# Perceiver layers: how the softmax sums of the last two head groups are joined in the two context attentions

## The chip, the cores and the metric

The kernel runs on one core of one Trainium2 chip. The time is that of the device, in microseconds (us), for one execution; where several executions were timed, the median is given. The profile comes from one more execution, which the hardware profiler recorded.

## What is computed

Two perceiver layers work on 512 tokens of width 512 and on a context of 8192 rows of width 512, of which a key mask leaves a part. Each layer adds to x a cross attention from the tokens to the context (16 heads of width 32), a self attention, and a mixture of eight experts with two chosen. The change is in the cross attention alone, here called the context attention:

```python
x = x + _L0_xattn_ref(_layernorm(x, axis=-1), ctx_1024, mask_BxS2_bk0, ...)
x = x + _L0_attn_ref(_layernorm(x, axis=-1), ...)
x = x + _L0_ffn_ref(_layernorm(x, axis=-1), ...)
x = x + _L1_xattn_ref(_layernorm(x, axis=-1), ctx_1024, ctx_1024, mask_Bx1xSxS2_ik1, ...)
...
attn = jnp.einsum('bhid,bjhd->bhij', q, k)
attn = jnp.where(padding_mask[:, None, None, :], attn, -jnp.inf)
p = jax.nn.softmax(attn, axis=-1)
ctx = jnp.einsum('bhij,bjhd->bihd', p, v).reshape(b, s1, c)
out = ctx @ Wo.T + bo
```

## The kernel before

`attend_slots` does the context attention of one layer; it is built twice, once for each layer. The 16 heads make four groups of four heads (g = 0 to 3), and the keys that the mask leaves are gathered into n = 15 slots of 128 keys. The main part is a loop over 60 rounds, `at = 15 * g + i`, one for each group and slot. In this document a round is called by `at`: round 44 is the last slot of the third group (g = 2), rounds 45 to 59 are the last group (g = 3).

A round makes four score tiles, one for each head (`score`, TensorE, then `subtract`, which adds the negated row maxima, also on TensorE), and their exponentials (`exp`, ScalarE), which go into one tile `pT` of 128 keys by 4 heads by 512 queries. `accumulate` then multiplies the `pT` of an earlier round with the values (`acc`, TensorE). In the rounds before 41 the score maxima of the next group are worked out as well (`compare`, `take`); from round 41 on there are none, and `accumulate(2)` serves the round before the last one. For the first three groups each `acc` is a PSUM tile of its own, and VectorE adds it into `o` in SBUF (line 1052). For the last group all 15 slots sum up in one PSUM tile.

The softmax also needs the sum of `pT` over all keys. `add_up` adds the `pT` of up to four rounds into a tile `four`: on GpSimd (POOL) for the first three groups, on VectorE (DVE) for the last. What is left are the parts of a group: five for each of the first three groups (`four` of rounds 0-3, 4-7, 8-11, 12-13, and the `pT` of round 14), six for the last (three `four` and three `pT`). `denominators` multiplies each part with ones on TensorE, four matrix products for the four heads (line 1072), and they add up in the PSUM tile `den`. ScalarE turns `den` into its inverse as exp(-ln(den)) (lines 1078 and 1083; 202 and 203 in the last group).

`fillers` is a list of steps with the round from which they are due; one is taken at the end of each round. For the first three groups it holds `denominators` three rounds after the group's end, `divide` one later (GpSimd multiplies `o` with the inverse and adds the value bias, lines 1084 and 1086), and `outputs`, which multiplies `o` with the output weights (line 889) and has VectorE add the result to x (line 895). For the third group the outputs come in rounds 57 and 58.

The PSUM tiles of scores, `acc`, `den` and `ops` take their buffers in turn from seven (four tagged s, three tagged m), and before the last group from an eighth (tagged a, where the last group's `acc` then stays):

```python
k.tags = cycle("smsmsmsa")
...
                k.tags = cycle("smsmsms")
                acc = k.sums[g] = pacc.tile([P, S], F32, name="acc", tag="acc")
```

A tile can be written only when the last reader of the tile that held its buffer before is done. Each engine takes its instructions in the order in which the program was laid out. `pT` has five buffers, `four` five, `o` two.

Of the kernel before, what the change touches and what calls it, by code (L numbers as in the profile page):

```python
# [11 lines left out]
F32 = mybir.dt.float32  # L12
# [4 lines left out]
AF = mybir.ActivationFunctionType  # L17
ALU = mybir.AluOpType
# [3 lines left out]
P = 128  # L22
S = 512
# [6 lines left out]
NG = 4  # L30
# [35 lines left out]
def tile_perceiver(  # L66
# [5 lines left out]
    nc = tc.nc  # L72
# [127 lines left out]
    def inverse(to, src):  # L200

        nc.scalar.activation(to, src, AF.Ln)
        nc.scalar.activation(to, to, AF.Exp, scale=-1.0)
# [581 lines left out]
    def in_quads(pool, psum, pacc, qT, wo, bv, late, splits=None):  # L785
# [4 lines left out]
        k = SimpleNamespace(tags=cycle("ms"), ones32=ones[:, 0:HD], most={}, shifts={}, sums={}, o={}, d={}, bufs={"s": 3, "m": 3}, rowwise=False, negs={}, direct=(0,), later=(), last=NT - 1, lag=False, between=None)  # L790
# [54 lines left out]
        def begin(g):  # L845
            k.sums[g] = [pacc.tile([P, S], F32, name=name, tag=name) for name in ("acc", "den")]

        def divided(g, r, d, acc, den):
            inverse(d[:, r], den)
            nc.vector.tensor_tensor(k.o[g][:, r], acc, d[:, r], ALU.mult)  # L850
            if bv is not None:

                nc.scalar.activation(k.o[g][:, r], k.o[g][:, r], AF.Identity, bias=bv[:, g : g + 1])

        def finish_part(g, r, acc, den):

            if g not in k.o:
                k.o[g] = late().tile([P, S], F32, name="o", tag="o", bufs=2)
            divided(g, r, late().tile([P, S], F32, name="d", tag="d", bufs=1), acc, den)

        def finish(g, pieces=1):

# [31 lines left out]
                else:  # L894
                    nc.vector.tensor_tensor(x[:, t, :], x[:, t, :], ps, ALU.add)

        k.tile_s, k.subtract, k.shift_of = tile_s, subtract, shift_of
        k.begin, k.finish, k.finish_part, k.outputs, k.quotient = begin, finish, finish_part, outputs, quotient
        return k

# [18 lines left out]
    def attend_slots(pool, psum, pacc, kT, vN, qT, kbias, krow, wo, bv, late, keys, settle, values, unit, more, early, aside, beside, extra, plan, tail, phase=None):  # L919
# [6 lines left out]


        k = in_quads(pool, psum, pacc, qT, wo, bv, late, nc.gpsimd)
        k.bufs["s"] = 4
        k.rowwise = True  # L930
# [4 lines left out]
        tile_s, subtract, shift_of = k.tile_s, k.subtract, k.shift_of  # L935
        n = SLOTS

        def score(g, i, h, ps, stop):
            nc.tensor.matmul(  # L939
                ps, lhsT=kT[HD * h : HD * (h + 1), g, i * P : (i + 1) * P], rhs=qT[HD * h : HD * (h + 1), g, :],  # L940
                start=True, stop=stop,
            )

        whole = n * P // S
        rest = n * P - whole * S
# [80 lines left out]
        parts, dens = {g: [] for g in range(NG)}, {}  # L1026
# [3 lines left out]
        def accumulate(lag):  # L1030

            if len(behind) < lag:
                return
            g, i, pT = behind.pop(0)
            alone = g < NG - 1
            if alone:
                acc = tile_s(name="acc")
            elif i == 0:
                k.tags = cycle("smsmsms")
                acc = k.sums[g] = pacc.tile([P, S], F32, name="acc", tag="acc")  # L1040
            else:
                acc = k.sums[g]
            for h in range(GH):
                nc.tensor.matmul(  # L1044
                    acc[HD * h : HD * (h + 1), :], lhsT=vN[:, i, g * P + HD * h : g * P + HD * (h + 1)],
                    rhs=pT[:, h, :], start=alone or i == 0, stop=alone or i == n - 1,
                )
            if alone and i == 0:
                k.o[g] = late().tile([P, S], F32, name="o", tag="o", bufs=2)
                nc.scalar.copy(k.o[g], acc)  # L1050
            elif alone:
                nc.vector.tensor_tensor(k.o[g], k.o[g], acc, ALU.add)  # L1052

        def add_up(g, i, pT):

            engine = nc.gpsimd if g < NG - 1 else nc.vector
            if i % 4 == 0 or i >= (n - 1 if g < NG - 1 else (n - 1) // 4 * 4):
                parts[g].append(pT)
                return
            to = parts[g][-1]  # L1060
            if i % 4 == 1:
                to = late().tile([P, GH, S], F32, name="four", tag="four", bufs=5)
            engine.tensor_tensor(to, parts[g][-1], pT, ALU.add)  # L1063
            parts[g][-1] = to

        def denominators(g, which, end):

            for j in which:
                if j == 0:
                    dens[g] = tile_s(name="den")  # L1070
                for h in range(GH):
                    nc.tensor.matmul(
                        dens[g][HD * h : HD * (h + 1), :], lhsT=k.ones32, rhs=parts[g][j][:, h, :],
                        start=(j == 0), stop=(j == end - 1),
                    )
            if g < NG - 1:
                d = late().tile([P, S], F32, name="d", tag="d", bufs=1)
                nc.scalar.activation(d, dens[g], AF.Ln)
                dens[g] = d

        def divide(g):

            nc.scalar.activation(dens[g], dens[g], AF.Exp, scale=-1.0)
            nc.gpsimd.tensor_tensor(k.o[g], k.o[g], dens[g], ALU.mult)

            nc.gpsimd.tensor_scalar(k.o[g], k.o[g], bv[:, g : g + 1], None, ALU.add)

        def exp(pT, h, i, ps):
            nc.scalar.activation(pT[:, h, :], ps, AF.Exp, bias=kbias[:, i : i + 1])  # L1089

        for at in range(NG * n):
            g, i = divmod(at, n)
            mg, mi = divmod(at + n + lead, n)
            pT = late().tile([P, GH, S], F32, name="pT", tag="pT", bufs=5)
            if mg < NG:

                w, m = {}, {}
                for now, then in (((0, 1), (2, 3)), ((2, 3), (0, 1))):
                    for h in now:
                        w[h] = tile_s()  # L1100
                        score(g, i, h, w[h], False)
                    for h in then:
                        m[h] = tile_s(name="scm")
                        compare(mg, mi, h, m[h])
                    for h in now:
                        subtract(g, h, w[h])
                    for h in now:
                        exp(pT, h, i, w[h])
                    for h in then:
                        take(mg, mi, h, m[h])  # L1110
                accumulate(1)
                if mi == n - 1:
                    for j, f in zip((1, 3), shift_of(mg)):
                        fillers.append((at + j, f))
            else:
                tiles = [tile_s() for _ in range(GH)]
                for h in range(GH):
                    score(g, i, h, tiles[h], False)
                for h in range(GH):
                    subtract(g, h, tiles[h])  # L1120
                for h in range(GH):
                    exp(pT, h, i, tiles[h])
                accumulate(2)
            add_up(g, i, pT)
            if i == n - 1 and g < NG - 1:
                fillers.extend((
                    (at + 3, lambda g=g: denominators(g, range(len(parts[g])), len(parts[g]))),
                    (at + 4, lambda g=g: divide(g)),
                    (at + (13 if g == NG - 2 else 10), lambda g=g: k.outputs(g, (0, 1))),
                    (at + (14 if g == NG - 2 else 11), lambda g=g: k.outputs(g, (2, 3))),  # L1130
                ))
            behind.append((g, i, pT))
            fillers.sort(key=lambda f: f[0])
            if fillers and fillers[0][0] <= at:
                fillers.pop(0)[1]()
            if g == NG - 1 and i >= n - 2:

                lone = n - (n - 1) // 4 * 4
                whole = (n - 1) // 4
                end = whole + lone  # L1140
                denominators(g, range(0, whole - 1) if i == n - 2 else range(whole - 1, end - 2), end)
        accumulate(1)
        denominators(NG - 1, range(end - 2, end), end)
        accumulate(1)
        for _, f in fillers:
            f()
        for i in range(2):
            r = slice(i * S // 2, (i + 1) * S // 2)
            k.finish_part(NG - 1, r, k.sums[NG - 1][:, r], dens[NG - 1][:, r])
        k.outputs(NG - 1, range(NT))  # L1150

    def columns(pool, vector, tag):
# [1519 lines left out]
    for i in range(2):  # L2672
        nc.vector.tensor_tensor(worst, worst, overs[:, i : i + 1], ALU.max)
    n = nc.values_load(
        worst, min_val=0, max_val=2 * NKT,
        skip_runtime_bounds_check_because="a count of at most NKT, or that and NKT",
    )
    with tc.If(n > SLOTS):

        load_x()  # L2680
        with tile_pool(name="osb", bufs=1) as op:
            for i in range(2):
                o = op.tile([P, S], F32, name=f"osb{i}", tag=f"osb{i}")
# [5 lines left out]
        with tile_pool(name="osb1", bufs=1) as op:  # L2689
            for i in range(2):  # L2690
                o = op.tile([P, S], F32, name=f"osb1{i}", tag=f"osb1{i}")
# [113 lines left out]
```

## Time and profile before

| what | value |
|---|---|
| three timed runs | 1433.89, 1439.09, 1439.64 us (median 1439.09) |
| the profiled execution | 1441.17 us, of which the profile's span is 1439.5 us |
| mean granted TensorE clock | 0.992 |
| TensorE (PE) busy | 1402.9 us, 97% of the span |
| VectorE (DVE), ScalarE (ACT), GpSimd (POOL) busy | 696.0, 582.7, 425.4 us |
| context attention of layer 0, rounds 41 to 59 | about 335 to 394 us of the span |
| the same rounds in layer 1 | about 1095.6 to 1154.7 us |

Times in the views of the profile are microseconds from the span's start. A timeline row gives start, duration, engine, line, operation, tiles (output <- inputs), shape and count; in brackets stands how long the engine was idle before it and what ended that. A row of several instructions gives the time from the first's start to the last's end. A fp32 matrix product shows as two records, so the four products of one part are "x8". PE is the matrix products, PEld the weight loads beside them. PEclk is the clock that TensorE was granted, as a share of full speed.

### The profile page before, as it was taken

To read this page: it belongs to the slowest core of one execution; us is meant where nothing else is said; L and a number is where in the kernel's file an instruction comes from. 1 tells how busy PE (TensorE), PEld (TensorE's weight loads), DVE (VectorE), ACT (ScalarE), POOL (GpSimd) and SP (SyncE) were. 2 spreads that over 40 slices of the span, in tenths; PEclk is the share of its full clock that TensorE was granted. 3 is DMA by queue.
4 is the path that set the end of the run, shared out by engine and by line. 5 is a ranking of instruction groups with operands and counts; after the bars stand their busy time and mean duration, and the time that the engine had idled before them with its cause. 6 is when DMAs were issued, how large, how long until landed. Compare 5 with 4: busy or idle time off the path is not lost. (4 is left out here: it accounts for less than half of the span.)

```text
span 1439.5 us, 24959 instructions
## 1 busy us (share of the span) xinstructions
PE 1402.9 (97%) x9797; PEld 859.5 (60%) x9797; DVE 696.0 (48%) x1985; ACT 582.7 (40%) x1168; POOL 425.4 (30%) x359
## 2 busy tenths in 40 slices
PE   7989999999999999999999999999999999999997
PEld 3434444443244548999999766644434235499993
DVE  5558598985523524111111226768986525741112
ACT  2657476667723253111111121166667832411211
POOL 2151078987011110200001110058988010120002
PEclk9999999999999999999999999999999999999999
DMA  8554200000050005987888450000000050077574
GB/s 248 150 194 147 74 31 1 2 1 1 5 209 1 16 16 188 390 303 261 276 280 297 154 181 23 30 1 2 1 1 2 1 190 1 10 271 288 203 263 156
DMA packets 94267, 175.15 MB, mean 122 GB/s; under 512 B 5496, under 2 KB 32182, under 8 KB 92348
## 3 DMA queue, kind: packets, MB, share of 16 engines
q1 hardware_dynamic: 87004, 151.43, 31.4%
q0 software_dynamic: 6416, 19.94, 3.9%
q10 hardware_dynamic: 720, 2.10, 0.4%
q8 instruction: 79, 1.29, 0.4%
q14 instruction: 48, 0.39, 0.1%
HBM read 162.72 MB, written 9.68 MB: 120 GB/s over the span
## 5 line engine op out<-in xcount | busy, mean ns | idle before, releaser
L1089 ACT ACTIVATE pT<-sc,kbias 128x512 f32<-128x512 f32 x480 | 288.3, 707 | 95.9 <-PE sc L800 86.5
L968 DVE CUSTOM_DVE_ANT_0 masked<-scm,krowb 128x512 f32<-128x512 f32 (+2 forms) x400 | 213.8, 591 | 39.8 <-PE scm L957 38.2
L939 PE MATMUL sc<-qTf,kTf 32*128 32x512 f32 x960 | 216.6, 621 | 1.5 <-DVE tops L968 1.5
L2363 PE MATMUL hps<-tokens,w 128*128 128x160 f32 (+11 forms) x1408 | 193.3, 293 | 0.0
L957 PE MATMUL scm<-kTf,qTf 32*128 32x512 f32 (+2 forms) x800 | 188.9, 539 | 0.0
L2363 PEld LDWEIGHTS hps<-tokens,w 128*128 128x128 f32 x1408 | 184.1, 191 | 2.7 <-issue 1.0
L2384 PE MATMUL y<-hT,w 128*128 128x160 f32 (+11 forms) x1280 | 174.6, 295 | 0.0
L2384 PEld LDWEIGHTS y<-hT,w 128*128 128x128 f32 x1280 | 168.1, 191 | 2.5 <-issue 0.8
L1063 POOL TENSOR_TENSOR four<-four,pT 128x2048 f32<-128x2048 f32 x36 | 163.9, 4553 | 1.6
L939 PEld LDWEIGHTS sc<-qTf,kTf 32*128 32x128 f32 x960 | 73.6, 183 | 95.6 <-DVE tops L968 42.5
L1044 PE MATMUL acc<-pT,vNf 128*32 128x512 f32 x960 | 127.8, 604 | 0.0
L1063 POOL TENSOR_TENSOR four<-pT 128x2048 f32<-128x2048 f32 x24 | 109.3, 4555 | 54.1 <-ACT pT L1089 54.1
L968 DVE CUSTOM_DVE_ANT_0 masked<-sc,krowb 128x512 f32<-128x512 f32 (+2 forms) x176 | 98.4, 614 | 55.4 <-PE sc L957 55.0
L2615 DVE TENSOR_TENSOR hT<-sg,hps 128x264 f32<-128x264 f32 (+7 forms) x64 | 27.9, 436 | 192.4 <-ACT sg L2614 191.0
L2614 ACT ACTIVATE sg<-hps 128x264 f32<-128x264 f32 (+7 forms) x64 | 25.3, 396 | 174.5 <-PE hps L2363 169.7
L957 PEld LDWEIGHTS scm<-kTf,qTf 32*128 32x128 f32 x800 | 86.1, 184 | 15.4 <-issue 6.2
L800 PE MATMUL sc<-shift,ones 3*128 3x512 bf16 (+3 forms) x544 | 93.3, 368 | 0.0
L2415 POOL DMA_DIRECT2D answers_d<-yb x17 | 9.6, 564 | 238.7 <-ACT yb L2402 233.0
L1052 DVE TENSOR_TENSOR o<-o,acc 128x512 f32<-128x512 f32 x84 | 57.3, 682 | 20.5 <-PE acc L1044 20.5
L1044 PEld LDWEIGHTS acc<-pT,vNf 128*32 128x32 f32 x960 | 19.3, 108 | 70.3 <-DVE tops L968 34.7
L1233 PE MATMUL pv<-wkvf,cslot 128*128 128x512 f32 x120 | 55.4, 611 | 3.1 <-DMA wq<-in_L_xattn_WqT 1.9
L1421 PE MATMUL pk<-cslot,wkf 128*128 128x256 f32 (+1 forms) x256 | 55.5, 370 | 0.0
(391 smaller groups left out, 1833.0 us busy)
## 6 DMA issues: line engine op xcount, KB each, us to landing
w<-in_L_ffn_W SPq DMA_DIRECT2D x94, 1024.0 KB, 5.3
mi<-in_mask SPq DMA_DIRECT2D x32, 512.0 KB, 4.6
cslot<-in_ctxT SPq DMA_DIRECT2D x40, 256.0 KB, 4.0
answers_d<-yb POOLq DMA_DIRECT2D x13, 256.0 KB, 4.6
answers_d<-zero POOLq DMA_DIRECT2D x9, 256.0 KB, 3.1
wkvf<-in_L_xattn_WkvT SPq DMA_DIRECT2D x8, 256.0 KB, 6.6
wof<-in_L_xattn_WoT SPq DMA_DIRECT2D x2, 1024.0 KB
wide<-in_L_attn_wk SPq DMA_DIRECT2D x4, 512.0 KB, 5.9
```

Source lines behind the costliest of these rows:

```text
L800: nc.tensor.matmul(ps, lhsT=ones16[r, :], rhs=k.shifts[g][r, 0:w], start=start, stop=stop)
L939: nc.tensor.matmul(ps, lhsT=kT[HD * h : HD * (h + 1), g, i * P : (i + 1) * P], rhs=qT[HD * h : HD * (h + 1), g, :], start=True, stop=stop,)
L957: nc.tensor.matmul(ps[:, at : at + w], lhsT=qT[HD * h : HD * (h + 1), g, t * P : (t + 1) * P], rhs=kT[HD * h : HD * (h + 1), g, lo : lo + ...
L968: nc.vector.tensor_tensor_reduce(masked[:, 0:w], ps[:, at : at + w], krow[:, lo : lo + w], 1.0, -BIG, ALU.add, ALU.max, accum_out=tops[g % ...
L1044: nc.tensor.matmul(acc[HD * h : HD * (h + 1), :], lhsT=vN[:, i, g * P + HD * h : g * P + HD * (h + 1)], rhs=pT[:, h, :], start=alone or i ...
L1052: nc.vector.tensor_tensor(k.o[g], k.o[g], acc, ALU.add)
L1063: engine.tensor_tensor(to, parts[g][-1], pT, ALU.add)
L1089: nc.scalar.activation(pT[:, h, :], ps, AF.Exp, bias=kbias[:, i : i + 1])
L1233: last = nc.tensor.matmul(ps.rearrange("p (g n) -> p g n", g=NG), lhsT=src[:, c, s % 2, :], rhs=wkv[:, :, c, i * P : (i + 1) * P], start=( ...
L1421: end = nc.tensor.matmul(ps[:, j], lhsT=wk[:, g, c], rhs=src[:, c], start=(c == 0), stop=(c == NC - 1))
L2363: end = nc.tensor.matmul(ps[:, j, 0:k], lhsT=w1[:, c, f * P : (f + 1) * P], rhs=tokens[:, c, starts[r] : starts[r] + k], start=(c == 0), s ...
L2384: nc.tensor.matmul(accs[0][:, d, 0:k], lhsT=w2[:, f, d * P : (d + 1) * P], rhs=hT[:, f, 0:k], start=(c == 0 and f == 0 and d % 2 == 0), st ...
```

## The change

For the third group (g = 2): right after its last round, VectorE adds the last `pT` into the fourth `four` and then the first `four` into the second (`join`), so that three parts are left in place of five. Its `denominators` are due four rounds after the group's end in place of three, and its `divide` five in place of four. Its quotient is multiplied on VectorE and its bias added on ScalarE, where both were GpSimd's.

For the last group: VectorE joins the first two `four` after slot 7, the sum and the third `four` after slot 11, and adds the `pT` of slot 12 as well, so that three parts are left in place of six. `denominators` no longer runs in rounds 58 and 59; all of it comes at the end, the two lone `pT` before the last `acc` and the `four` after it. The inverse is taken of both halves first, and then both are multiplied.

In the layout of the built program nothing else moves. On VectorE the two joins of the third group stand after the first of its last three additions of `acc` into `o`, and ahead of the other two.

```diff
         def add_up(g, i, pT):
-            engine = nc.gpsimd if g < NG - 1 else nc.vector
-            if i % 4 == 0 or i >= (n - 1 if g < NG - 1 else (n - 1) // 4 * 4):
+            final = g == NG - 1
+            if i % 4 == 0 and not (final and i >= n - 3) or i >= n - (2 if final else 1):
                 parts[g].append(pT)
                 return
...
-            engine.tensor_tensor(to, parts[g][-1], pT, ALU.add)
+            (nc.vector if final else nc.gpsimd).tensor_tensor(to, parts[g][-1], pT, ALU.add)
             parts[g][-1] = to
+            if final and i in (n // 2, n - 4):
+                join(g, 1, 0)
+
+        def join(g, to, of):
+            ins = nc.vector.tensor_tensor(parts[g][to], parts[g][to], parts[g][of], ALU.add)
+            parts[g].pop(of)
+            return ins
...
         def divide(g):
             nc.scalar.activation(dens[g], dens[g], AF.Exp, scale=-1.0)
+            if g == NG - 2:
+                nc.vector.tensor_tensor(k.o[g], k.o[g], dens[g], ALU.mult)
+                nc.scalar.activation(k.o[g], k.o[g], AF.Identity, bias=bv[:, g : g + 1])
+                return
             nc.gpsimd.tensor_tensor(k.o[g], k.o[g], dens[g], ALU.mult)
...
             add_up(g, i, pT)
+            if i == n - 1 and g == NG - 2:
+                joined = join(g, 3, 4)
+                with tc.issue_after(joined.ins):
+                    join(g, 1, 0)
             if i == n - 1 and g < NG - 1:
+                rest = 4 if g == NG - 2 else 3
                 fillers.extend((
-                    (at + 3, lambda g=g: denominators(g, range(len(parts[g])), len(parts[g]))),
-                    (at + 4, lambda g=g: divide(g)),
+                    (at + rest, lambda g=g: denominators(g, range(len(parts[g])))),
+                    (at + rest + 1, lambda g=g: divide(g)),
...
-            if g == NG - 1 and i >= n - 2:
-                lone = n - (n - 1) // 4 * 4
-                whole = (n - 1) // 4
-                end = whole + lone
-                denominators(g, range(0, whole - 1) if i == n - 2 else range(whole - 1, end - 2), end)
         accumulate(1)
-        denominators(NG - 1, range(end - 2, end), end)
+        denominators(NG - 1, (1, 2), True, False)
         accumulate(1)
+        denominators(NG - 1, (0,), False, True)
...
         for i in range(2):
-            r = slice(i * S // 2, (i + 1) * S // 2)
-            k.finish_part(NG - 1, r, k.sums[NG - 1][:, r], dens[NG - 1][:, r])
+            inverse(d[:, r[i]], dens[NG - 1][:, r[i]])
+        for i in range(2):
+            k.divided(NG - 1, r[i], d[:, r[i]], k.sums[NG - 1][:, r[i]])
         k.outputs(NG - 1, range(NT))
```

More of the change, by code (lines that the diff above doesn't have):

```diff
@@ L846, in begin, with divided @@
             k.sums[g] = [pacc.tile([P, S], F32, name=name, tag=name) for name in ("acc", "den")]
-        def divided(g, r, d, acc, den):
-            inverse(d[:, r], den)
-            nc.vector.tensor_tensor(k.o[g][:, r], acc, d[:, r], ALU.mult)
+        def divided(g, r, d, acc):
+            nc.vector.tensor_tensor(k.o[g][:, r], acc, d, ALU.mult)
             if bv is not None:
@@ L858, in finish_part @@
                 k.o[g] = late().tile([P, S], F32, name="o", tag="o", bufs=2)
-            divided(g, r, late().tile([P, S], F32, name="d", tag="d", bufs=1), acc, den)
+            d = late().tile([P, S], F32, name="d", tag="d", bufs=1)
+            inverse(d[:, r], den)
+            divided(g, r, d[:, r], acc)
         def finish(g, pieces=1):
@@ L895, in outputs @@
                     nc.vector.tensor_tensor(x[:, t, :], x[:, t, :], ps, ALU.add)
-        k.tile_s, k.subtract, k.shift_of = tile_s, subtract, shift_of
+        k.tile_s, k.subtract, k.shift_of, k.divided = tile_s, subtract, shift_of, divided
         k.begin, k.finish, k.finish_part, k.outputs, k.quotient = begin, finish, finish_part, outputs, quotient
@@ L1062, in add_up, with denominators @@
                 to = late().tile([P, GH, S], F32, name="four", tag="four", bufs=5)
-            engine.tensor_tensor(to, parts[g][-1], pT, ALU.add)
+            (nc.vector if final else nc.gpsimd).tensor_tensor(to, parts[g][-1], pT, ALU.add)
             parts[g][-1] = to
-        def denominators(g, which, end):
+            if final and i in (n // 2, n - 4):
[4 more added lines that the diff above has]
+            return ins
+        def denominators(g, which, first=True, last=True):
+            if first:
+                dens[g] = tile_s(name="den")
             for j in which:
-                if j == 0:
-                    dens[g] = tile_s(name="den")
                 for h in range(GH):
@@ L1073, in denominators @@
                         dens[g][HD * h : HD * (h + 1), :], lhsT=k.ones32, rhs=parts[g][j][:, h, :],
-                        start=(j == 0), stop=(j == end - 1),
+                        start=first and j == which[0], stop=last and j == which[-1],
                     )
@@ L1135, in attend_slots @@
                 fillers.pop(0)[1]()
-            if g == NG - 1 and i >= n - 2:
-                lone = n - (n - 1) // 4 * 4
-                whole = (n - 1) // 4
-                end = whole + lone
-                denominators(g, range(0, whole - 1) if i == n - 2 else range(whole - 1, end - 2), end)
         accumulate(1)
-        denominators(NG - 1, range(end - 2, end), end)
+        denominators(NG - 1, (1, 2), True, False)
         accumulate(1)
+        denominators(NG - 1, (0,), False, True)
         for _, f in fillers:
             f()
+        r = slice(0, S // 2), slice(S // 2, S)
+        d = late().tile([P, S], F32, name="d", tag="d", bufs=1)
+        k.o[NG - 1] = late().tile([P, S], F32, name="o", tag="o", bufs=2)
         for i in range(2):
-            r = slice(i * S // 2, (i + 1) * S // 2)
-            k.finish_part(NG - 1, r, k.sums[NG - 1][:, r], dens[NG - 1][:, r])
+            inverse(d[:, r[i]], dens[NG - 1][:, r[i]])
+        for i in range(2):
+            k.divided(NG - 1, r[i], d[:, r[i]], k.sums[NG - 1][:, r[i]])
         k.outputs(NG - 1, range(NT))
```

## The prediction

> **What bounds the kernel now.** I read the page first: TensorE is busy 97% of the span, so only what changes TensorE's own work or makes it wait can move the end.
>
> ```profile
> PE 1402.9 (97%) x9797; PEld 859.5 (60%) x9797; DVE 696.0 (48%) x1985; ACT 582.7 (40%) x1168; POOL 425.4 (30%) x359
> ...
> L1063 POOL TENSOR_TENSOR four<-pT 128x2048 f32<-128x2048 f32 x24 | 109.3, 4555 | 54.1 <-ACT pT L1089 54.1
> ```
>
> The second row matters later: one addition of 128x2048 takes 4.56 us on POOL; on DVE it takes 2.29 (timeline below). Then the timeline of layer 0 around the end of the third group. Layer 1 has the same rows 760.6 us later, to within 0.1, so every term below counts twice.
>
> ```profile
> 344.54 4.55 POOL L1063 TENSOR_TENSOR four<-pT 128x2048 f32<-128x2048 f32 x1
> 344.64 1.14 PE L939 MATMUL sc<-qTf,kTf 32*128 32x512 f32 x8
> 344.78 0.69 DVE L1052 TENSOR_TENSOR o<-o,acc 128x512 f32<-128x512 f32 x1 [1.87 <-PE acc L1044]
> ...
> 347.06 0.69 DVE L1052 TENSOR_TENSOR o<-o,acc 128x512 f32<-128x512 f32 x1 [1.60 <-PE acc L1044]
> ...
> 349.21 1.14 PE L939 MATMUL sc<-qTf,kTf 32*128 32x512 f32 x8
> 349.35 0.69 DVE L1052 TENSOR_TENSOR o<-o,acc 128x512 f32<-128x512 f32 x1 [1.60 <-PE acc L1044]
> 350.17 0.40 PE L800 MATMUL sc<-shift,ones 3*128 3x512 bf16 x4
> 350.50 1.07 PE L1044 MATMUL acc<-pT,vNf 128*32 128x512 f32 x8
> ...
> 355.79 1.14 PE L939 MATMUL sc<-qTf,kTf 32*128 32x512 f32 x8
> 355.92 0.60 ACT L1078 ACTIVATE d<-den 128x512 f32<-128x512 f32 x1 [2.80 <-PE den L1072]
> ```
>
> The scores at 344.64, 349.21 and 355.79 open rounds 45, 47 and 48. A round without extras is 2.29 us of TensorE (346.93 to 349.21), and the five parts of `den` take 355.79 - 351.50 = 4.29 us, 0.857 each. POOL's last addition ends at 349.09: until then VectorE cannot join that tile. Third, the tail of layer 0.
>
> ```profile
> 382.85 1.98 PE L889 MATMUL ops<-wof,o 128*128 128x512 f32 x4
> 384.01 0.69 DVE L895 TENSOR_TENSOR x<-x,ops 128x512 f32<-128x512 f32 x1 [2.20 <-PE ops L889]
> ...
> 391.37 1.90 PE L1072 MATMUL den<-pT,ones 128*32 128x512 f32 x16
> 393.08 1.04 PE L1044 MATMUL acc<-pT,vNf 128*32 128x512 f32 x8
> 393.47 0.38 ACT L202 ACTIVATE d<-den 128x256 f32<-128x256 f32 x1 [2.99 <-PE den L1072]
> ```
>
> TensorE runs through it without a gap, so each part of `den` lies on the path. Last, the windows around three places where TensorE waits today (length, PE, PEld, DVE, ACT, POOL busy, granted clock, DMA):
>
> ```profile
> 88.70:93.38 4.68, 0.05 (x2) 0.01 (x1) 0.75 (x2) 3.78 (x11) 1.12 (x4) 0.89 0.20 16
> 93.38:99.18 5.80, 5.80 (x15) 2.55 (x16) 4.87 (x15) 4.05 (x10) 0.43 (x2) 0.50 0.88 270
> ...
> 585.75:587.33 1.58, 0.01 (x1) 0.00 (x0) 0.43 (x1) 0.39 (x1) 0.00 (x0) 1.00 1.06 395
> 587.33:592.00 4.67, 4.14 (x35) 3.93 (x36) 0.00 (x0) 1.16 (x2) 0.00 (x0) 1.00 1.02 400
> 1424.85:1427.06 2.21, 0.00 (x1) 0.00 (x0) 1.54 (x3) 0.37 (x1) 0.00 (x0) 0.98 0.09 35
> 1427.06:1430.40 3.34, 3.34 (x4) 1.51 (x5) 0.69 (x1) 0.00 (x0) 0.00 (x0) 0.50 0.02 7
> ```
>
> After 4.6 us without work the clock is halved for 5.8 us of work, after 2.2 us for 3.3 us, after 1.6 us not at all.
>
> **The change, part by part (per layer, times of layer 0).**
>
> *What it removes.* Third group: two of five parts of `den`, -2 x 0.857 = -1.71 us of TensorE. Last group: three of six parts, -3 x 0.857 = -2.57. Both lie on the path. POOL's product and bias (1.29 + 1.56 us at 357.26) leave an engine that nothing waits for until round 57: nothing.
>
> *What the joins queue up.* On DVE the two joins stand behind the addition at 344.78 and ahead of those at 347.06 and 349.35. The first needs POOL's tile: it starts at about 349.15. Two additions at a pitch of 2.35 (dependent ones started 2.40 apart at 350.91 and 353.31; a merged pair takes 4.69) end at about 353.85; the delayed addition of `acc` ends at 354.5 instead of 347.75. That addition is the last reader of a PSUM buffer. Counting the buffers from the start of the loop (400 tiles before round 45, so `smsmsmsa` begins anew there), round 45's `acc` is its fifth tile, an s; the fourth s after it is the third score of round 47. So TensorE, which takes its queue in order, stands at that score from 349.5 (349.21 and two of four scores) until 354.55: **+5.05**. Behind it wait two scores, the shifts, the products with the values, and ScalarE's exponentials of rounds 47 and 48. Only an earlier end on POOL could shorten this, and POOL's chain is unchanged. The later due round of `den` costs nothing: the joins are over at 353.85, `den` comes after round 48 at about 358.9.
>
> *The quotient on DVE and ACT.* After the exponential of `den`, ACT now waits for DVE's product (as 0.69 for 128x512) and adds the bias (0.60, as line 1078), with hand-overs 1.4 us, ahead of round 49's exponentials. DVE's product is queued behind the fourth `four` addition, which needs round 48's `pT` (done 360.35) and so ends at 362.8, just when the inverse is ready. TensorE has round 49 and three scores of round 50 to run meanwhile; the fourth needs a buffer that round 49's first exponential frees. It would come at 364.1, the buffer at 364.95: +0.85. From then ACT's pace rules (0.578 us for each of 40 exponentials in 23.22 us, 2.31 a round against 2.29), +0.15 until round 57. Together **+1.0**, with bounds 0 (hidden) and 1.4 (nothing hidden).
>
> *The longer chain of additions.* From round 52's exponentials DVE now has seven additions in a row (slot 7, join, slots 9, 10, 11, join, slot 12), 7 x 2.35 = 16.5 us, then x <- x,ops: 17.2 with hand-over. This addition was at 380.54, before; in DVE's order it now comes after the chain. The second `ops` product of round 58 reuses the first `ops` buffer of round 57 (seven tiles on). TensorE reaches it 15.0 us after round 52's exponentials today (368.8 to 383.8) and some 14.8 then: **+2.4** (bounds 0, if the additions do not run on end, and 3.0, at the 2.40 pitch with TensorE's round at 2.29).
>
> *The order at the end.* `den` now ends after the last `acc`, not before: ScalarE starts its logarithm one part later against TensorE's end, **+0.86**. Both logarithms before both exponentials puts the first half's quotient 0.4 later and the second's 0.8 earlier; the first statistics start at 396.51 today, right behind the second quotient, so I count +0.2. In layer 0 the next stage's first product (400.92) starts 0.7 after its input is copied, so some 0.5 is absorbed there.
>
> Sum per layer without the clock: -1.71 - 2.57 + 5.05 + 1.0 + 2.4 + 0.86 + 0.2 = +5.2; both layers, less 0.5: **+10.0**.
>
> *The clock.* The first stall leaves TensorE idle for 4.6 us (349.9, when two heads' scores drain, to 354.55). By the rows at 93.38 and 1427.06 that costs half of 5.8 or of 3.3 us: 2.9 or 1.7. I take 2.2, between them, since what opens the low stretch need not fall alike in both layers. The second stall, 2.4 us, lies between the rows of 1.6 (nothing) and 2.2 (1.7): I take half, 0.8. All of it is TensorE's time while ScalarE waits for it. Both layers: 2 x 3.0 = **+6.0**.
>
> [...]
>
> The profiled execution took 1441.17 us (span 1439.5): 1441.2 + 16 = 1457.2. It lies 2.1 above the median of the three runs, so against the median 1439.09 I predict **1455**.
>
> **The rivals.**
>
> *The joins do no harm and the parts are saved.* This ends on the other side. It needs the additions of `acc` not to be held at POOL's 349.09, or PSUM buffers to last: if the stalls (first, quotient, second, clock) together stay below 1.71 + 2.57 - 0.86 - 0.2 = 3.2 us a layer, the change gains. With none of them it is -6.4: 1432.7. Against it: POOL's row is back to back with the one before it, so its end is no accident. Chance 0.10 (a gain of over 0.5% needs the reorder to cost nothing as well, 1430.5).
>
> *The stalls come, the clock holds.* Then +10.0, 1449. For it: the gap at 585.75 left the clock at 1.00. Against it: that gap is a third as long. Chance 0.20.
>
> *The clock is low longer.* With 2.9 and 1.7 in both layers +19.2: 1458. Chance 0.15.
>
> My forecast, the first stall with one low stretch each, has 0.55.
>
> **How the numbers follow.** The range reaches from below the second rival to beyond the third: 1444 (the second, with the quotient hidden and the second stall at half, 1449 - 2.0 - 2.4 = 1444.6) to 1462 (the third with the upper bounds of quotient and second stall, 2 x (0.4 + 0.6) more, 1460, and 2 for the median: the runs before spread over 5.8). A measurement of this kernel can tell about 0.5% (7.2 us) from no change. Faster by more: 0.04. Within it: the rest of the first rival, 0.06, and the lower edge of the second, 0.02. Slower: 0.88.
>
> **What would show it.** Right: in both layers the third score of round 47 waits about 5 us for an addition of `acc`, VectorE's two joins stand right before it with a wait for POOL ahead, and the granted clock reads 0.50 for some us after. `den` of the third group is "x24" in place of "x40". `ops` in round 58 waits for x <- x,ops. Wrong: scores of round 47 at the old pace, or an `acc` addition before the joins; PEclk at 1.00 behind the stall would put the time at the second rival.

## The result, and the profile after

The changed kernel takes 1458.30 us (median of four runs, 1454.53 to 1460.36) against 1439.01 (four runs as well): a ratio of 1.0137, 95% interval 1.012 to 1.0154. It is slower, as forecast, and 3.3 us above the forecast of 1455. The profiled execution has a span of 1457.5 us at a mean granted clock of 0.984 (0.992 before). The page's first row, for the whole span:

```profile
PE 1409.8 (97%) x9717; PEld 862.1 (59%) x9717; DVE 719.0 (49%) x1997; ACT 584.2 (40%) x1170; POOL 420.9 (29%) x355
```

TensorE has 80 products fewer (9797 before), the five parts of two layers, and is yet busy for 6.9 us more, in part because products took longer where the granted clock read 0.50 (the scores of a round 2.09 us at 360.17, 1.14 at 348.53). Where it stood still is in the view of what TensorE waited for (total, times, longest). The first two rows were not there before; the third read 0.3, 2, 0.2:

```profile
PE sc L940 <- DVE o L1053: 7.8, 2, 3.9
...
PE ops L890 <- DVE x L896: 4.0, 2, 2.0
...
PE ops L890 <- ACT o L852: 2.0, 2, 1.0
```

The timeline of layer 0 shows the first wait. Lines are one or a few higher than before: 940 is the score, 1053 the addition of `acc` into `o`, 1071 a join, 896 the addition into x.

```profile
346.14 4.55 POOL L1064 TENSOR_TENSOR four<-pT 128x2048 f32<-128x2048 f32 x1
346.39 0.69 DVE L1053 TENSOR_TENSOR o<-o,acc 128x512 f32<-128x512 f32 x1 [1.87 <-PE acc L1045]
350.72 2.29 DVE L1071 TENSOR_TENSOR four<-four,pT 128x2048 f32<-128x2048 f32 x1 [3.65 <-ACT pT L1102]
350.82 1.13 PE L940 MATMUL sc<-qTf,kTf 32*128 32x512 f32 x4
352.93 2.28 DVE L1071 TENSOR_TENSOR four<-four 128x2048 f32<-128x2048 f32 x1
355.13 1.48 DVE L1053 TENSOR_TENSOR o<-o,acc 128x512 f32<-128x512 f32 x2
355.87 1.22 PE L940 MATMUL sc<-qTf,kTf 32*128 32x512 f32 x2 [3.92 <-DVE o L1053]
```

VectorE adds one `acc` at 346.39 and idles 3.65 us until GpSimd's last addition ends (346.14 + 4.55 = 350.69; the row's bracket names ScalarE, whose exponentials of that round were done before). It makes two joins, and only then adds the other two `acc`, whose products had ended at 348.6 and 350.9. TensorE issues two of the four scores of round 47 at 350.82; the third would follow 0.28 later and starts at 355.87, 4.77 us late. Layer 1 has the same (1120.38 and 1125.40: 4.74 late).

The windows of the same execution (length, PE, PEld, DVE, ACT, POOL busy, granted clock, DMA) show what follows each wait in layer 0:

```profile
352.00:355.60 3.60, 0.00 (x0) 0.00 (x0) 3.60 (x3) 0.42 (x1) 0.00 (x0) 1.00 0.00 0
355.60:362.40 6.80, 6.53 (x28) 1.54 (x28) 4.99 (x4) 2.42 (x4) 0.00 (x0) 0.50 0.00 0
362.60:366.00 3.40, 3.40 (x36) 0.88 (x32) 1.05 (x2) 2.42 (x4) 0.00 (x0) 1.00 0.00 0
...
396.60:400.00 3.40, 3.40 (x20) 0.97 (x24) 0.68 (x1) 0.96 (x2) 0.00 (x0) 0.50 0.00 0
```

The clock is halved just as TensorE gets its buffer, stays there for 6.8 us, and again for 3.4 us after the second wait (of the second `ops` product of round 58, 2.02 us, over at 395.43).

**An account by stage.** Single executions differ by several us in stages that the change does not touch (1315.4 to 1322.9 us of the profiled executions lie outside the two stages, see e2), so I compare the kernels by the stage alone: from VectorE's copy of the last row maxima (`shift<-stp`, in the third group's last round; 342.50 before, 344.10 after) to the first weight load of the next stage (`vps`; 400.89 before, 412.40 after). "Lost" is TensorE's busy time multiplied by one minus the granted clock, summed over half-microsecond windows. "Timed" is the ratio of the timed runs with its interval, in us of a median of 1437.5 for before. The rows below the second are the experiments.

| kernel | timed, us against before | stage in layer 0, 1 | against before, both layers | lost to the clock, layer 0, 1 |
|---|---|---|---|---|
| before | 0 | 58.39, 59.53 | 0 | 0, 0 |
| after | +19.7 (17.3 to 22.1) | 68.30, 68.64 | +19.0 | 4.98, 4.22 |
| e1_third_joins | +15.2 (12.9 to 17.4) | 64.93, 66.70 | +13.7 | 3.42, 4.06 |
| e2_quotient | +5.9 (4.0 to 7.6) | 59.73, 60.86 | +2.7 | 0, 0 |
| e3_last_group | +5.5 (3.3 to 7.8) | 58.99, 61.76 | +2.8 | 0, 1.68 |
| e4_kept_busy | +13.2 (10.1 to 16.5) | 65.40, 66.59 | +14.1 | 1.71, 1.71 |
| e5_late_joins | +5.2 (3.3 to 7.0) | 59.73, 60.85 | +2.7 | 0, 0 |
| e6_outputs_first | +10.9 (8.8 to 13.2) | 64.96, 66.03 | +13.1 | 3.94, 3.88 |
| e7_all_moved | -5.2 (-7.2 to -3.2) | 55.36, 56.70 | -5.9 | 0, 0 |
| e8_joins_swapped | +35.9 (33.4 to 38.7) | 64.54, 65.76 | +12.4 | 3.42, 3.42 |
| e9_swapped_held | +15.8 (12.2 to 19.4) | 67.44, 69.05 | +18.6 | 4.28, 4.75 |
| e10_late_joins_alone | -4.2 (-5.9 to -2.4) | 57.17, 58.51 | -2.2 | 0, 0 |

### The profile page after: what moved, and what is told of

It is laid out like the page before. It is cut to its first block, busy times and chain, and to the rows that moved or that the text cites. A ratio compares the mean times of both kernels' runs of the same rounds, so it can differ in the third digit from the quotient of the medians.

```text
span 1457.5 us, 24792 instructions
## 1 busy us (share of the span) xinstructions
PE 1409.8 (97%) x9717; PEld 862.1 (59%) x9717; DVE 719.0 (49%) x1997; ACT 584.2 (40%) x1170; POOL 420.9 (29%) x355
## 4 chain that ended last, share of the span: by engine, by line
PE 80%; DVE 5%; issue 3%; ACT 2%; DMA 2%; POOL 1%; DVEq 0%; POOLq 0%; SPq 0%; ACTq 0%
PE hps L2380 11%; PE y L2401 11%; PE sc L940 9%; PE acc L1045 7%; PE prj L1629 4%; PE pk L1438 4%; PE scm L958 4%; PE ops L890 3%; PE sc L958 2%; PE pva L1565 2%; PE pv L1250 2%; DVE four L1064 2%; PE sc L800 2%; PE den L1081 2%; PE y L2357 1%
## 5 line engine op out<-in xcount | busy, mean ns | idle before, releaser
L940 PE MATMUL sc<-qTf,kTf 32*128 32x512 f32 x960 | 226.2, 638 | 9.5 <-DVE o L1053 7.8
L800 PE MATMUL sc<-shift,ones 3*128 3x512 bf16 (+3 forms) x544 | 96.7, 376 | 0.0
L1053 DVE TENSOR_TENSOR o<-o,acc 128x512 f32<-128x512 f32 x84 | 57.3, 683 | 14.3 <-PE acc L1045 14.1
L1709 DVE TENSOR_REDUCE neg<-sc 128x1 f32<-128x512 f32 (+3 forms) x64 | 26.9, 484 | 58.5 <-PE sc L1705 58.5
```

The source lines that it names most:

```text
L800: nc.tensor.matmul(ps, lhsT=ones16[r, :], rhs=k.shifts[g][r, 0:w], start=start, stop=stop)
L940: nc.tensor.matmul(ps, lhsT=kT[HD * h : HD * (h + 1), g, i * P : (i + 1) * P], rhs=qT[HD * h : HD * (h + 1), g, :], start=True, stop=stop,)
```

## The experiments

**The three parts of the change, each alone.** e1 is the kernel before with the third group's joins:

```diff
             add_up(g, i, pT)
+            if i == n - 1 and g == NG - 2:
+                joined = join(g, 3, 4)
+                with tc.issue_after(joined.ins):
+                    join(g, 1, 0)
...
-                    (at + 3, lambda g=g: denominators(g, range(len(parts[g])), len(parts[g]))),
-                    (at + 4, lambda g=g: divide(g)),
+                    (at + (4 if g == NG - 2 else 3), lambda g=g: denominators(g, range(len(parts[g])), len(parts[g]))),
+                    (at + (5 if g == NG - 2 else 4), lambda g=g: divide(g)),
```

> The kernel before with only the third group's two joins on VectorE, its three parts, and its den and divide one round later; the quotient stays on GpSimd and the last group keeps its four parts as before. Theory (the joins in front of two o additions cost a stall of TensorE and a clock drop behind it): per layer -1.71 us for two parts saved, +4.8 us of stall, +3.4 us of half clock, in all +6.5; both layers +13, so about 1452 us (1447 to 1455), with the wait of a score for the o addition in the PE waits at about 3.9 us twice. Rival that the stall costs but the half clock belongs to other parts of the change: about +6, 1445 us. Rival that the joins are harmless and the time went in the last group: -3.4 us, about 1435.6 us.

Measured 1452.99 us, ratio 1.0106 (1.009 to 1.0121); the score waits for the `o` addition 7.8 us in two times, as in after. Per layer +6.54 and +7.17 for an expected +6.5. The joins alone carry most of the loss, with their half clock.

e2 is the kernel before with the third group's quotient moved:

```diff
             nc.scalar.activation(dens[g], dens[g], AF.Exp, scale=-1.0)
+            if g == NG - 2:
+                nc.vector.tensor_tensor(k.o[g], k.o[g], dens[g], ALU.mult)
+                nc.scalar.activation(k.o[g], k.o[g], AF.Identity, bias=bv[:, g : g + 1])
+                return
             nc.gpsimd.tensor_tensor(k.o[g], k.o[g], dens[g], ALU.mult)
```

> The kernel before with only the third group's quotient on VectorE and its bias on ScalarE. Theory (a small term): 0 to +0.7 us per layer (one ScalarE bias of 0.72 us between the exps), so 1439 to 1440.5 us and no new wait over 0.5 us on TensorE. Rival that this move carries a good part of the 19 us (exps pushed back, a new stall of the scores): 1443 us or more.

Measured 1442.53 us, ratio 1.0041 (1.0028 to 1.0053): more than I expected. The stage is 1.34 and 1.33 us longer. The timeline of e2 shows it on ScalarE and TensorE:

```profile
358.19 0.72 ACT L1086 ACTIVATE o<-o,bvC 128x512 f32<-128x512 f32 x1 [0.76 <-DVE o L1085]
...
358.32 1.91 PE L939 MATMUL sc<-qTf,kTf 32*128 32x512 f32 x7
...
360.07 0.59 PE L939 MATMUL sc<-qTf,kTf 32*128 32x512 f32 x1
```

ScalarE waits 0.76 us for VectorE's product and works 0.72 on the bias, and the exponentials begin that much later. A round's last score, which needs a buffer that they free, is issued 1.2 us late (that round takes 3.48 us between its products with the values, 357.33 to 360.81, in place of 2.29); the rest is ScalarE's pace in the rounds after it, 2.31 us each. The view of waits has no row for it, because the wait lies inside a group of eight that TensorE had begun. Nothing of the move is hidden.

The timed +5.9 is more than the stage's +2.7, and so it is with e3 and e5. Most of the rest is the clock elsewhere. Outside the two stages the profiled executions took between 1315.4 us (e3) and 1322.9 (e1), e8 aside, and lost between 3.9 us (e3) and 11.9 (e5) of it to the clock; without that loss all of them lie between 1309.7 and 1311.8. In the timed runs the mean granted clock is lower than in their runs of before by 0.0013 for e2 and 0.0030 for e3 and e5, which is about 2 and 4 us of such a span. Why the clock was low there more often stays open.

e3 is the changed kernel with the third group put back, that is the last group's part alone:

```diff
-            if i == n - 1 and g == NG - 2:
-                joined = join(g, 3, 4)
-                with tc.issue_after(joined.ins):
-                    join(g, 1, 0)
...
-                rest = 4 if g == NG - 2 else 3
+                rest = 3
...
-            if g == NG - 2:
-                nc.vector.tensor_tensor(k.o[g], k.o[g], dens[g], ALU.mult)
-                nc.scalar.activation(k.o[g], k.o[g], AF.Identity, bias=bv[:, g : g + 1])
-                return
```

> The changed kernel with the third group as before (no joins, five parts, quotient on GpSimd): the last group's part alone. Theory: per layer -2.57 us for three parts saved, +0.86 us for the part that stands last, +0.2 us for the order of the inverses, +2.0 us for the third output product that waits for VectorE's chain, and 0 or +1.7 us of half clock behind that wait; in all +0.5 to +2.2 per layer, so 1440 to 1443.5 us, the wait of ops for the x addition still 2.0 us. Rival that the last group's part brings its saving: about 1434 us. Rival that this part holds most of the loss: over 1449 us.

Measured 1441.11 us, ratio 1.0038 (1.0023 to 1.0054). Per layer +0.60 and +2.23, of which 0 and 1.68 are clock; `ops` waits for x 2.1 us in each layer. The saving of three parts, -2.57, is eaten by that wait and the late part. The three parts of the change add up: 13.7 + 2.7 + 2.8 = 19.2 for the 19.0 of the whole.

**The clock by itself.** e4 keeps TensorE busy in the stall:

```diff
                 tiles = [tile_s() for _ in range(GH)]
+                if at == (NG - 1) * n + 2:
+                    for f in range(16):
+                        pin(nc.tensor.matmul(tiles[0][:, 0:P], lhsT=ident, rhs=ident, start=(f == 0), stop=(f == 15)))
                 for h in range(GH):
```

> The changed kernel with 16 products of the 128x128 identity with itself ahead of the scores of the third round of the last group (0.21 us each by the 0.857 us of a 128x512 part, 3.4 us in all): they fill the time in which TensorE stood still behind the joins and are overwritten by the score. Theory: the third score starts when it did, since VectorE frees its buffer as before; TensorE is idle for about 1.4 us instead of 4.8 us and the clock stays at 1.00 there, so 3.4 us per layer come back, about 1451.5 us (1449 to 1453). Rival that the half clock does not come from that idle time: the clock drops as before and the time stays at 1458 us. Rival that TensorE was not free there: the products add their 6.8 us, 1465 us.

Measured 1451.19 us, ratio 1.0092 (1.007 to 1.0115). The timeline, and then a window, of e4 in layer 0:

```profile
349.64 3.84 PE L1132 MATMUL sc<-ident 128*128 128x128 f32 x32
353.41 1.13 PE L940 MATMUL sc<-qTf,kTf 32*128 32x512 f32 x4
354.71 0.70 PE L940 MATMUL sc<-qTf,kTf 32*128 32x512 f32 x2 [0.17 <-DVE o L1053]
```

```profile
354.60:362.40 7.80, 7.69 (x64) 2.52 (x68) 6.68 (x5) 5.00 (x9) 0.00 (x0) 1.00 0.00 0
```

The third score starts 5.07 us after this round's place in TensorE's queue (349.64 to 354.71; in after 350.82 to 355.87, 5.05): the stall is the same, but filled. The granted clock stays at 1.00, and the stage is 2.90 and 2.05 us shorter than in after. More work on TensorE made the kernel faster; this is the clock's part shown by itself. The loss of 1.71 that is left in each layer comes from the second wait, which in layer 1 of after had cost nothing.

**Taking the waits away.** e5 makes the joins from within `accumulate`, behind the third group's last addition into `o`, with `rest` 5 in place of 4:

```diff
-                nc.vector.tensor_tensor(k.o[g], k.o[g], acc, ALU.add)
+                added = nc.vector.tensor_tensor(k.o[g], k.o[g], acc, ALU.add)
+                if g == NG - 2 and i == n - 1:
+                    with tc.issue_after(added.ins):
+                        joined = join(g, 3, 4)
+                    with tc.issue_after(joined.ins):
+                        join(g, 1, 0)
```

> The changed kernel with the third group's joins behind the last o addition on VectorE (ordered by an edge), its den and divide one round later again. Theory: no score waits for an o addition any more, stall (4.8 us) and half clock (3.4 us) of each layer are gone: 1458.3 - 16.4 = about 1442 us (1439 to 1445). Rival that the joins only hand the wait on (the last group's sums start 4.5 us later on VectorE, the five pT buffers run out and exps and scores wait): over 1450 us.

Measured 1443.25 us, ratio 1.0036 (1.0023 to 1.0049). The wait of the score for the `o` addition is gone from the view of waits and the clock stays at 1.00 in both stages: -8.57 and -7.79 us per layer against after. The long wait did not move on, but a short one came, which after has not:

```profile
PE sc L940 <- ACT pT L1107: 1.7, 2, 0.9
```

In each layer a score waits 0.86 us for an exponential behind the quotient's bias (366.25 in layer 0). The stage is 1.2 us longer than the other terms of the change add up to (-4.28 + 1.34 + 2.02 + 1.07 = +0.15; measured +1.34 and +1.32 against before), and two rounds account for it: one takes 2.79 us between its products with the values (353.33 to 356.12) in place of 2.29, as in e7 below, and the one with the wait takes 4.26 (363.26 to 367.52), where e2 took 3.48.

e6 lets the four additions into x go ahead of the second join and slot 12:

```diff
+            if final and i == n - 3:
+                return
...
-            if final and i in (n // 2, n - 4):
+            if final and i == n // 2:
...
+            if at == NG * n - 2:
+                with tc.issue_after(k.stored.ins):
+                    joined = join(g, 1, 0)
+                with tc.issue_after(joined.ins):
+                    nc.vector.tensor_tensor(parts[g][0], parts[g][0], behind[-2][2], ALU.add)
```

(`k.stored` is the last addition into x, `behind[-2][2]` the `pT` of slot 12.)

> The changed kernel with the four x additions of the third group's output products ahead of the last group's second join and of slot 12's sum on VectorE (ordered by edges). Theory: the wait of ops for the x addition (2.0 us) and the half clock behind it in one layer (1.7 us) are gone: 1458.3 - 4.0 to - 5.7 = 1452.6 to 1454.3 us. Rival that the last den then waits for the two sums as long as ops did before: 1458 us.

Measured 1449.05 us, ratio 1.0076 (1.0061 to 1.0092), below the range that I expected. The wait of `ops` for x is gone; the stage is 3.34 and 2.61 us shorter than in after, 5.95 in both layers, just above my upper end of 5.7. The timed runs differ by 9.25; in the profiles e6 also lost 4.3 us less than after to the clock outside the stages (6.4 against 10.7). The last `den` does not wait longer for it.

e7 is e5 and e6 together, with the quotient back on GpSimd:

> The changed kernel with the joins behind the last o addition, the x additions ahead of the second join, and the quotient back on GpSimd: all three waits taken away while the five parts fewer per layer stay. Theory: -4.28 us of parts, +0.86 us for the part that stands last, +0.2 us for the order of the inverses: -3.2 us per layer, about 1432.6 us (1430 to 1436), clock as in the kernel before. Rival that the parts were hidden beside other work and their saving never reaches the end: about 1439 us.

Measured 1433.64 us, ratio 0.9964 (0.995 to 0.9978): faster than both kernels. The stages are 3.03 and 2.83 us shorter than before, for an expected 3.2. The timeline of e7 where the stall was:

```profile
353.21 0.69 DVE L1053 TENSOR_TENSOR o<-o,acc 128x512 f32<-128x512 f32 x1 [1.60 <-PE acc L1045]
353.82 2.28 DVE L1078 TENSOR_TENSOR four<-four,pT 128x2048 f32<-128x2048 f32 x1
356.02 2.28 DVE L1078 TENSOR_TENSOR four<-four 128x2048 f32<-128x2048 f32 x1
```

The joins follow the last addition of `acc`, and the additions into `o` keep the old pace of a round.

e10 is the kernel before with e5's late joins and nothing else (`den` due at +5, `divide` at +6):

> The kernel before with the third group's two joins behind the last o addition, its three parts, its den two rounds later, and nothing else (quotient on GpSimd, last group with its four parts as before). Theory: -1.71 us per layer for two parts saved and no new wait; both layers -3.4 us, about 1434 us, clock 1.00 throughout this stage. Rival that the saved parts were hidden, or that joins on VectorE cost as much wherever they stand: 1437 us or more.

Measured 1434.5 us, ratio 0.9971 (0.9959 to 0.9983). The stages are 1.22 and 1.02 us shorter, not quite 1.71. In e7 one round near the joins takes 2.79 us between its products with the values (354.36 to 357.15) in place of 2.29, because the round's fourth score is late, and e10 has the same. The view of waits has no row for it, but the trace's semaphore events put the first product of that score (355.88 in e7, 352.58 in e10) down to an exponential that had just ended (355.83 and 352.53). So it is ScalarE that holds it, as in e2: here it works without a pause, 24 exponentials from 347.47 to 361.94 in e7. That half microsecond is about what e10 falls short by (0.49 and 0.69).

**The order of the joins: two misses.** e8 is the changed kernel with the joins swapped:

```diff
-                joined = join(g, 3, 4)
+                joined = join(g, 1, 0)
                 with tc.issue_after(joined.ins):
-                    join(g, 1, 0)
+                    join(g, 2, 3)
```

> The changed kernel with the two joins in the other order: first the one whose two parts were ready long ago, then the one that waits for GpSimd's last sum and the last exps. Theory: the first join falls into VectorE's idle 3.65 us, one addition of 2.2 us no longer lies between GpSimd's end and the o additions, the stall is 2.6 us instead of 4.8 us, and the half clock behind it is one window of at most 1.7 us lost, or none: 2.2 to 5.6 us less per layer, 1447 to 1454 us. Rival that the stall hangs on the last sum alone, not on the number of additions in front: 1458 us.

Measured 1474.97 us, ratio 1.025 (1.0232 to 1.0269), the slowest of all. Its timeline in layer 0:

```profile
329.92 2.29 DVE L1071 TENSOR_TENSOR four<-four 128x2048 f32<-128x2048 f32 x1 [6.82 <-POOL four L1064]
332.95 1.22 PE L940 MATMUL sc<-qTf,kTf 32*128 32x512 f32 x1 [6.62 <-DVE tops L969]
...
362.60 2.29 DVE L1071 TENSOR_TENSOR four<-four,pT 128x2048 f32<-128x2048 f32 x1 [3.63 <-ACT pT L1102]
365.55 0.70 PE L940 MATMUL sc<-qTf,kTf 32*128 32x512 f32 x2 [1.70 <-DVE o L1053]
```

With no edge to hold it, the layout of the program put the free join six `o` additions earlier on VectorE, amid the scans for the row maxima. There it waits 6.82 us for GpSimd, and a score whose buffer a scan has yet to read waits 6.62: the same mechanism as in the change, in a worse place. It lies ahead of the stage's start, so the stage shows only 12.4 of the 35.9 us. The stall under study did shrink as expected: the third score is 2.55 us late (365.55 against 362.72 + 0.28), one addition less than 4.77. So the length of the stall is the work queued ahead of the `o` additions.

e9 holds the first join in its place:

```diff
+                with tc.issue_after(k.added.ins):
+                    joined = join(g, 1, 0)
                 with tc.issue_after(joined.ins):
-                    join(g, 1, 0)
+                    join(g, 2, 3)
```

(`k.added` is the `o` addition ahead of the joins.)

> The changed kernel with the two joins in the other order, each held by an edge: the join of the two parts that were ready long ago stands behind the o addition that came ahead of both joins, so that it can't slip further forward, and the join that waits for GpSimd's last sum and the last exps follows it. Theory (the stall is the VectorE work that lies between the arrival of the last part and the o additions): the first join falls into the idle 3.65 us, the stall is one addition shorter, 4.8 - 2.2 = 2.6 us per layer, and the half clock behind it costs 0 to 3.4 us; so 2.2 to 5.6 us less per layer than the changed kernel, 1446 to 1453 us, and the wait of the score for the o addition about 1.7 us instead of 3.9 us. Rival that the last part alone sets it: 1457 us.

Measured 1455.24 us, ratio 1.011 (1.0085 to 1.0135), and the wait is 3.8 us, not 1.7. Its timeline:

```profile
344.77 4.55 POOL L1064 TENSOR_TENSOR four<-pT 128x2048 f32<-128x2048 f32 x1
345.61 5.86 DVE L1071 TENSOR_TENSOR four<-four 128x2048 f32<-128x2048 f32 x1
351.39 2.28 DVE L1071 TENSOR_TENSOR four<-four,pT 128x2048 f32<-128x2048 f32 x1
353.60 1.47 DVE L1053 TENSOR_TENSOR o<-o,acc 128x512 f32<-128x512 f32 x2
354.32 1.22 PE L940 MATMUL sc<-qTf,kTf 32*128 32x512 f32 x2 [3.76 <-DVE o L1053]
```

The free join starts in VectorE's idle time and takes 5.86 us in place of 2.29 (5.84 in layer 1). GpSimd's addition ends at 349.32, the join 2.15 later, which is nearly the 2.29 us of a whole addition (in layer 1 at 1116.37, and 2.14 later). I had not expected that; by what the one addition holds up the other, no run shows. So the idle 3.65 us ahead of the joins were not there to be used.

## Why the prediction was right, point by point

Per layer, with what the runs showed for each term (layer 0, layer 1 where they differ):

| term | predicted | measured | shown by |
|---|---|---|---|
| five parts fewer | -4.28 | -4.28 (as counted) | `den` x24 (363.43) for x40; e7 and e10 gain, somewhat less than counted |
| first stall | +5.05 | +4.77, +4.74 | timeline; e5 removes it |
| quotient on VectorE and ScalarE | +1.0 | +1.34, +1.33 | e2 |
| second stall | +2.4 | +2.02, +2.00 | waits; e6 removes it |
| last part after the last `acc`, and order of inverses | +1.06 | +1.07 | e3: 0.60 + 2.57 - 2.1; first `ops` waits 1.03 for ScalarE, 0.17 before |
| half clock | +3.0 | +4.98, +4.22 | clock windows; e4 |
| sum | +8.2 | +9.9, +9.1 | stages: +9.91, +9.11 |

**Where it held.** The mechanism of the first stall was the right one in each step: the two joins ahead of two `o` additions, the buffer of round 45's `acc`, the third score of round 47. The size is 0.28 too high because I took VectorE's pitch from additions that depend on each other (2.40) or merged ones (2.35); the two joins are independent and start 2.21 apart. These are the dependent ones, in the profile before:

```profile
350.91 2.29 DVE L1063 TENSOR_TENSOR four<-pT 128x2048 f32<-128x2048 f32 x1 [0.88 <-ACT pT L1089]
353.31 2.29 DVE L1063 TENSOR_TENSOR four<-four,pT 128x2048 f32<-128x2048 f32 x1
```

The second stall came where it was placed. Its 2.4 rested on seven additions at a pitch of 2.35 and measured 2.0. The +1.06 of the tail fits to 0.01 as a sum; the 0.5 that I let layer 0 absorb was not absorbed, since layer 0's terms sum to 9.90 without it and its stage is 9.91 longer. That the terms without the clock come to 9.8 us in both layers, for 10.0 forecast, is in part luck: the errors of the two stalls (-0.28 and -0.38 a layer), of the quotient (+0.34) and of the 0.5 nearly cancel.

**Where it was off.** The clock term is the one that was mis-sized: 6.0 predicted, 9.2 measured for both layers. The step that failed is "I take 2.2, between them". The gap of 4.6 us had a row of its own length (88.70: 5.8 us at half clock) and a row half as long (1424.85: 3.3 us); the mean gave the short gap the same weight. Even the long one alone would have given too little: its low stretch was 6.83 us (92.37 to 99.20), of which 1.0 fell into the gap. Behind the first stall TensorE was idle for only 3.9 us, not 4.6, and the low stretch was 6.83 us in layer 0 and 10.24 in layer 1 (1123.60 to 1133.84, of which 1.8 fell into the wait). There the clock cost 3.27 in layer 0 (4.98 less the 1.71 of the second) and 4.22 in layer 1. For the second stall half of 1.7 was assumed, and it fell once, in layer 0, and not in layer 1: the mean that was predicted. So the case that came true is, by its number, the third rival (clock low longer, +19.2, 1458), to which I gave 0.15, and not the likeliest one; it differs from that in this one term.

The quotient was taken at 1.0 with 1.4 as the bound for "nothing hidden". e2 puts it at that bound: the 0.85 that I counted for the late buffer was 1.2.

**The rivals that fell.** "The joins do no harm" needed the additions of `acc` not to be held at GpSimd's end, and they were held beyond it. But its price was right about the parts: with the three waits away e7 gains 5.9 us in the two stages, for 6.4 counted. "The clock holds" falls with the windows, and e4 shows what it would have been worth.

## What to carry to other kernels

An addition that is free on an engine at half load is not free in that engine's queue: ask what stands behind it, and whether that releases a PSUM buffer that TensorE needs next. Put such work behind the releases and hold it there with an edge, because the layout may put a free instruction much earlier (e8, where one join lacked the edge and went six additions forward, took 16.7 us more than the changed kernel). And price each wait of TensorE twice, once for itself and once for the clock after it: here 4.8 us of waiting cost 3.3 to 4.2 more.

## What the runs showed of the hardware that was not expected

- **How long the clock stayed halved did not follow from the length of the gap.** After the same wait of 3.9 us, 3.27 us were lost in layer 0 and 4.22 in layer 1; after the same 2.0 us, 1.71 in one layer and nothing in the other; and e8's wait of only 1.70 us was followed by 3.42 lost in layer 0 (0.50 from about 366.4 to 373.2), a low stretch of 6.83 us, and 1.71 in layer 1. In the records of the granted clock each low stretch of the two stages lasts 3.41, 6.83 or 10.24 us, one to three times 3.41, and the same wait of 3.9 us brings 6.83 (layer 0 of after and e1) or 10.24 (layer 1 of both, both layers of e6). A low stretch also came nearly without a wait: in the profile before, TensorE is busy for 4.79 of the 5.10 us up to 1263.1, and the clock reads 0.50 for the 6.8 us after it. What opens a low stretch, and what ends it, the runs do not show.
- **Beside GpSimd's addition VectorE's join of two tiles showed as one long instruction, not as idle time**: 5.86 and 5.84 us in e9, where 2.29 is usual, ending 2.15 and 2.14 us after GpSimd's. `o<-o,acc`, which has one input in PSUM, took its usual 0.69 beside GpSimd (347.06 in the profile before, with GpSimd's addition from 344.54 to 349.09).
- Two additions of 128x2048 on VectorE started 2.21 us apart where they were independent (350.72 and 352.93 in after), and 2.40 (350.91 and 353.31 in before) or 2.33 (387.76 and 390.09 in after) where the second read the result of the first.
